# A second matrix product by one level of Strassen, softmax sums taken from the exponentials, and a new order table, in a fused graph-attention and slice-attention layer

## The chip, the cores and the metric

The kernel runs on one core of a Trainium2 chip. The metric is the device time of one execution in microseconds (us); the time before is the median of three runs. TensorE (PE) multiplies matrices out of SBUF into eight PSUM banks; its weight loads have a row of their own (PEld). VectorE (DVE) and ScalarE (ACT) do the elementwise work, GpSimd (POOL) a little, and SyncE (SP) issues nearly all transfers (DMA). Each engine runs its instructions in the order in which they are written.

## The reference, cut to what matters

There are 32 batches of 512 tokens with 256 features, all float32. A graph-attention block and a slice-attention block are each added to their input:

```python
# graph block on xn = layernorm(x)
out = relu(xn @ mlp1_w + mlp1_b)                  # 256 -> 512
residual = out
out = elu(gat(relu(out), None, W_fc, a_fc)) + residual
out = relu(out @ mlp2_w + mlp2_b)                 # 512 -> 256, the second mlp
residual = out
out = relu(elu(gat(relu(out), adj, W_hand, a_hand)) + residual)
x = x + out
# gat: h = inp @ W; e = leaky_relu(h @ a1 + (h @ a2).T), masked by adj; elu(softmax(e) @ h)

# slice block on xn2 = layernorm(x), 8 heads, 64 slices
slice_weights = softmax((x_mid @ W_slice + b_slice) / temp)   # over the 64 slices
slice_token = (fx_mid.T @ slice_weights) / sum(slice_weights)
attn = softmax(q @ k.T * scale); out_slice = attn @ v
x = x + (out_slice spread by slice_weights) @ W_out + b_out
```

## The kernel before, in words

Each batch goes through `front` (first layer norm, first mlp, first attention), `middle` (second mlp, second attention, residual) and `back` (second norm, slice softmax, slice attention, output). A batch is small, so the batches are pipelined: while one batch is in `back`, others are in `front` and `middle`, and their instructions are interleaved on every engine.

The interleaving is computed when the kernel is built. `nc` is a `Recorder` (line 105): every operation is noted with its engine, an estimated cost (`_cost`, line 182) and the tiles that it reads and writes. `_schedule` (line 226) then lets the engines take their next operation one by one, at each moment the one with the lowest key that could start, and respects data dependences and the number of buffers of each tag. The key (`order`, line 314) is `age * PERIOD + turn + shift`: `age` is the batch, `turn` comes from `TURNS`, which has a row of numbers for each step of the code (`nc.step = "mlp2"` and so on), and `shift` from `HEAD` and `TAIL`, which move whole steps of the first and last three batches. `SETUP` orders the preparation of the weights. `emit` (line 332) writes the instructions out in that order, and so each engine's queue has a fixed order. All recorded instructions therefore carry line 343 in the profile. Only in the first and last 120 us (in estimated time) does `emit` add fill matmuls on the identity (line 351) where TensorE would wait.

The steps that the change and the prediction touch:

- **The first attention** (`h` and `pv`, lines 761 to 902) already uses one level of Strassen in its two large products. There `product` makes one of seven products in a PSUM bank, and VectorE adds them up (`total`), with two copies by ScalarE (`keep`). `mix` and `pmix` hold the mixed operands.
- **o1** (line 902): the result comes back from a transposition by DMA into `o1T` (features on partitions, tokens on the free axis), and VectorE adds the residual.
- **mlp2** (line 912): `o2T = relu(w2.T @ o1T + b2)`, 256 features in two blocks of 128. Each block is four matmuls of 128 x 128 by 512 tokens, accumulated in one bank, then one ReLU with bias by ScalarE out of PSUM. The matmuls read `o1T` through `swapped` (line 477), which permutes the tokens on the way.
- **h2, e, p2, pv2** (lines 922 to 1008): the second, masked attention. `h2` projects `o2T`; `f2b` spreads one of the logits over a row; VectorE forms the masked rows `e` with their maxima `top`, ScalarE the exponentials, VectorE the maximum of both; the rows go out by `e_stage` and come back transposed in `p2T`. `pv2` multiplies and adds the residual into `x1`. `o2T` also goes out through `o2_stage`.
- **norm2** (line 1046): the second layer norm. The transposed rows come back by DMA into `xn2_raw`, which is a tile of the tag `o2T`: the same single buffer as the second mlp's output. ScalarE copies it into `xn2T`. (The profile shows the two names as `xn_raw` and `xn2T`.)
- **w** (line 1061): slice softmax. For each of four tiles of 128 tokens: logits of 512 columns in PSUM, the maximum of each of the 8 heads by VectorE (`mx`), 8 exponentials of 64 columns by ScalarE, the sums `rs` of the heads by a VectorE reduction over the 512 columns, their reciprocals, and a product.

In the first and last batch the transpositions are done by TensorE and not by DMA (`by_dma`, line 459), and `f2b` is copied out of PSUM.

Of the kernel before, what the change touches and what calls it, by code (L numbers as in the profile page):

```python
# [10 lines left out]
AF = mybir.ActivationFunctionType  # L11
OP = mybir.AluOpType
AX = mybir.AxisListType
# [1 line left out]
ENGINES = ("tensor", "vector", "scalar", "gpsimd", "sync")  # L15

TURNS = {
    "load": (-104.13,),
    "norm1": (5.81, -12.2, -0.38, 40.46, 5.49, 6.82, -28.3, -97.35, 73.26, 2141.3, -17.24, 7.8,
        -3.21, -61.78, -29.05, -31.03, -34.36, -3.93, -211.23, -208.37, -208.62, -207.57,  # L20
        -202.44),
    "mlp1": (44.88, -14.78, 475.5, -0.81, 29.84, 144.85, 30.48, 28.34, 46.7, 63.76, 30.7,
        163.15),
    "h": (217.43, 239.71, 301.88, 219.38, 228.31, 232.52, 223.78, 123.55, -183.63, -198.06,
        235.55, 281.78, 134.23, 84.93, 296.28, 284.15, 228.15, 213.81, 208.35, 40.76, -192.43,
        -208.97, 324.43, 90.08, 232.1, 162.36, 264.44, 305, 269.96, 302.11, 159.39, 131.88,
        217.06, 97.44, 286.09, 265.51, 197.21, 172.48, 330.83, 139.13, 316.66, 332.6, 199.8,
        210.03, 184.56, 233.17, 252.5, 357.26, 288.33, 243.5, 272.56, 242.46, 243.89, 262.61,
        301.12, 303.21),
    "factors": (1172.98, 68.61, 957.87, 880.81, 833.88, -94.89, 162.9, 564.16, 443.05, 632.16,  # L30
        99.22, 41.55, 117.2, -36.09, 151.35, 166.12, 162.03),
    "p": (-217.52, 222.09, -214.68, 156.3, -232.9, 226.84, -201.59, 222.19),
    "pv": (181.62, 173.02, 113.17, 168.75, 130.31, 121.86, 154.04, 91.05, 128.61, 93.43, 156.55,
        170.07, 249.5, 203.18, 183.65, 209.43, 161.93, 146.07, 129.44, 175.77, 84.33, 98.64,
        193.99, 67.43, 82.92, 77.34, 188.5, 225.33, 179.85, 196.17, 141.96, 66.83, 209.82,
        122.72, 185.96, 166.17, 256.1, 208.95, 191.25, 109.15, 168.68, 33.05, 111.29, 31.79,
        223.06, 225.68, 0.25, 146.41, 143.11, 131.52, 150.56, 135.14, 171.77, 185.87, 148.08,
        129.9, 112.28, 230.93, 210.68, 202.98, 108.67, 123.15, 135.98, 121.57, 427.87, 287.12,
        306.19, 126.95, 47.96, 44.6, 23.6, 354.94, 212.32, 233.37, 145.94, -25.73, 89.65, 87.01,
        301.3, 340.74),  # L40
    "o1": (175.72, 146.36, 318.31, 75.22, 202.48, -123.71, -11.06, -130.7, -287.11),
    "mlp2": (163.2, 216.89, 255.93, 271.92, 60.63, 285.36, 184.81, 130.74, 28.96, 65.99),
    "h2": (154.01, 126.18, 171.55, 124.34, 108.59, 78.41, 169.3, 89.79, 186.32, 157.35, 180.91,
        192.19, 105.96, 124.57, 26.13, 58.76),
    "e": (226.55, 172.24, 227.68, 199.08, 187.7, 234.17, 190.31, 206.45, 237.64, 232.92, 168.72,
        256.08, 408.52, 421.68, 391.27, 262.45, 442.54, 455.27, 273.82, 234.38, 519.53, 170.71,
        164.48, 31.36),
    "p2": (-14.68, 22.01, 55.59, 61.1, 56.92, -11.8, 67.6, 558.07, 85.28, 48.17, 40.53, 30.86,
        19.78, -12.55),
    "pv2": (231.3, 86.58, 94.48, 97.84, -101.11, 186.76, 109.51, 61.52, 85.01, -131.77, -150.14,  # L50
        205.52, 259.66, 267.31, 237.42, -131.44, -160, -120.69, -132.24, 154.68, 148.6, 111.83,
        139, -129.21, 152.77, 106.35, 144.25, 119.14, -162.13, -156.66, 273.74, 322.31, 325.93,
        361.68, -139.88, -151.25, -142.85, -161.55),
    "norm2": (3024.02, 107.62, 108.82, 88.2, 97.55, 53.73, 74.18, 49.61, 117.29, 3167.28,
        180.18, 68.34, 64.85, 86, 21.41, 8.51, 60.74, 13.84, 28.42, 83.96, 129.51, 212.73,
        234.97, 261.11, 2822.4, 116.47),
    "w": (305.34, 272.53, 290.14, 845.93, 798.64, 795.47, 283.65, 884.75, 926.27, 320.18, 751.4,
        375.01, 408.12, 405.42, 336.46, 305.77, 323.75, 367.7, 1201.11, 1138.46, 1563.38,
        745.63, 1124.55, 865.97, 1179.02, 980.75, 363.54, 428.69, 395.78, 437.6, 334.39, 367.5,
        367.07, 981.88, 934.2, 840, 174.53, 1035.96, 203, 1037.78, 1034.98, 480.9, 411.92,  # L60
        442.36, 358.87, 346.56, 246.11, 386.64, 1234.45, 758.39, 808.64, 610.85, 681.86, 882.99,
        492.47, 722.21, 414.99, 446.77, 335.28, 249.32),
    "sums": (219.1, 219.58, 227.77, 239.7, 383.95, 249.92, 251.57, 239.42, 242.03, 1077.37,
        1977.83, 234.3, 1454.25, 735.43, 2640.86, 592.26, 423.25, 660.64, -9.73),
    "s1T": (108.57, 368.64, 346.43, 140.99, 183.21, 126.3),
    "tokens": (328.88, 276.03, 298.43, 280.34, 354.01, 226.15, 295.4, 216.36, 344.5, 310.56,
        213.27, 259.2, 166.72, 280.67, 245.65, 277.29, 211.49, 312.02, 299.07, 271.19, 138.52,
        257, 235.11, 203.31, 251.8, 264.98, 212.57),
    "att": (205559.95, 208057.13, 394.33, 51833.74, 297.35, 190333.7, 260689.92, 418216.35),
    "vo": (374.47, 235.14, 638.61, 320.05, 321.87, 373.17, 345.11, 230.64, 163.72, 211.34,  # L70
        232.93, 232.76, 169.48, 276.17, 419.48, 556.46),
    "gg": (-50.95, -63.34, -63.34, -51.08, -78.74, -66.07, -40.3, -20.46, 150.92, 121.98),
    "out": (158.85, 78.08, -2.92, 6.88, -44.11, -73.16, -25.26, -4.67, 103.63, 87.34, -10.37,
        24.58, -12.49, 48.01, 59.4, 101.43, 136.08, 81.21, 268.69),
}
PERIOD, SPARE = 80.54, 0.01

HEAD = (
    (-61, -359, 0, 40, 0, 69, -1262, 189, -43, 457, -8, -24, 143, 947, 108, 718, -48, 6, 1, -39,
     119, -20),  # L80
    (168, 1, 0, 0, 0, 4, 174, 0, 144, -26, 75, 433, 58, 166, 0, 117, 154, 0, -183, -48, -372,
     1721),
    (172, 728, 1325, 0, -59, -269, -21, 34, -18, -363, 2035, 398, 404, -24, 1613, -199, 25,
     -134, 0, -3, -46, -85),
)
TAIL = (
    (36, 0, -352, 1, 67, 0, -772, 105, -24, 0, -312, 50, -6, -235, 1896, 375, 54, 83, -211, 13,
     -147, -271),
    (18, -170, -262, -383, 0, 42, 11, -11, -950, 795, -14, -10, -1671, -108, -157, 653, 6, 18,
     0, 210, 2, 652),  # L90
    (-4, -40, 0, -69, 10, -43, -630, -53, 276, -593, -1, -10, -589, 151, 299, 42, 316, 15, 89,
     4, -160, 43),
)


SETUP = (791.3598735632129, 2808.359873563213, 4385.359873563213, 9205.359873563213, 6407.359873563213, 3020.359873563213, 4840.359873563213, 5931.359873563213)

FLIPPED = ("xn", "u", "e", "o2", "w", "xn2")

P = 128  # L100
# [290 lines left out]
def adj_ffn_kernel(  # L391
# [26 lines left out]
    B, N, D = x.shape  # L418
    HID = mlp1_w.shape[1]
    HH = HID // 2  # L420
    NT = N // P
    KD = D // P
    KH = HID // P
    HEADS = temperature.shape[1]
# [12 lines left out]
    def ts(i, n=P):  # L437
        return slice(i * n, (i + 1) * n)

    def new(name, shape, bufs=1, tag=None, dtype=F32):  # L440
        return sbuf.tile(list(shape), dtype, name=name, tag=tag or name, bufs=bufs)

    def mm_tile(shape):
        return psum.tile(shape, F32, tag="bank", name="mm", bufs=8)
# [32 lines left out]
    def swapped(cols):  # L477

        return cols.rearrange("p (t a i) -> p a t i", t=NT, i=Q)
# [4 lines left out]
    def row(name, shape=(P, 512), tag=None):  # L484
        return new(name, shape, bufs=2, tag=tag)

    def small(name, shape):
        return new(name, shape, bufs=3)
# [74 lines left out]
    nc.step = "setup0"  # L563
    w2 = new("w2", [P, KH, D])
    nc.sync.dma_start(w2, mlp2_w.rearrange("(k p) f -> p k f", p=P))
    b2 = new("b2", [P, KD])
    nc.sync.dma_start(b2, mlp2_b.rearrange("(m p) -> p m", p=P))

# [341 lines left out]
    def middle(b, o1T):  # L910

        nc.step = "mlp2"
        o2T = new("o2T", [P, KD, N])
        for m in range(KD):
            pm = mm_tile([P, N])
            for k in range(KH):
                nc.tensor.matmul(
                    pm.rearrange("p (a t i) -> p a t i", t=NT, i=Q), w2[:, k, ts(m)],
                    swapped(o1T[:, k, :]), start=(k == 0), stop=(k == KH - 1),
                )  # L920
            nc.scalar.activation(o2T[:, m, :], pm, AF.Relu, bias=b2[:, m : m + 1])
        nc.step = "h2"
        h = new("h2", [P, NT, D + 2], tag="h" if b == B - 1 else None)
        for t in range(NT):
# [7 lines left out]
        for j in range(NT):  # L932
            nc.tensor.transpose(f2b[:, ts(j)], h[:, j, D + 1 : D + 2].to_broadcast([P, P]), ident)
        if not by_dma("e", b):
            pt, f2b = f2b, new("f2b", [P, N], tag="acb")
            nc.scalar.copy(f2b, pt)
        nc.step = "e"
        pT = new("p2T", [P, NT, N], tag="pT" if b == B - 1 else None)
# [105 lines left out]
    def back(b, x1):  # L1044
# [21 lines left out]
        for t in range(NT):  # L1066
# [7 lines left out]
            pm3 = pm.rearrange("p (h g) -> p h g", g=G)  # L1074
            mx = small("mx", [P, HEADS])
            nc.vector.tensor_reduce(mx, pm3, axis=AX.X, op=OP.max, negate=True)
            for hd in range(HEADS):
                nc.scalar.activation(w3[:, hd], pm3[:, hd], AF.Exp, bias=mx[:, hd : hd + 1])
            rs = small("rs", [P, HEADS])
            nc.vector.tensor_reduce(rs, w3, axis=AX.X, op=OP.add)  # L1080
            nc.vector.reciprocal(rs, rs)
            nc.vector.tensor_tensor(
                w3, w3, rs[:, :, None].to_broadcast([P, HEADS, G]), op=OP.mult
# [206 lines left out]
```

## Time and profile before

| | |
|---|---|
| Median of three runs | 2467.51 us (2467.47 to 2471.15) |
| The profiled execution, its own time | 2464.71 us |
| Its span, first to last instruction | 2462.9 us |
| Instructions in the span | 35296 |
| Granted TensorE clock, mean | 1.00 |
| ScalarE: exponentials of `w` | 1024 of 128 x 64, 231.1 us busy |
| Fill matmuls | 128 + 56 + 6, 26.1 us busy |
| TensorE busy before 374.58 us, and after 2167 us | 363.28 of 374.58, 287.27 of 295.90 us |

A span is counted from the first to the last instruction; a run's time is a little longer. In the lists of groups a line gives the code line, the engine, the operation, the tiles (out<-in), the shapes, the number of instructions, their busy time and mean duration in ns, and the idle time of the engine just before them with what ended it. A float32 matmul appears as two records, since it is made in two passes. In the list of instructions in order of time a line has the start in us, the length of the stretch in us, and then engine and tiles.

### The profile page before, as it was taken

Reading aid. Unit: us, or ns where it says so; the run is one execution under the profiler, and the core shown is the slowest. Engines: PE = TensorE matmul, PEld = TensorE weight load, DVE = VectorE, ACT = ScalarE, POOL = GpSimd, SP = SyncE. Lnnn points to the kernel's source line nnn. Section 1 sums busy time; section 2 is a strip of 40 time slices with the busy share of each in tenths; the row PEclk is TensorE's granted clock in tenths of the full one; section 3 lists DMA queues with packets and bytes.
Section 4 is the critical chain, followed back from the end, with each engine's and each line's share of the span. In section 5 each row is a group of like instructions: output and inputs, shape, how many; then the busy total and the mean of one; then the engine's idle time right before and its main releaser. Section 6 shows DMA issues by size and latency. Waiting matters only on the chain.

```text
span 2462.9 us, 35296 instructions
## 1 busy us (share of the span) xinstructions
PE 2442.5 (99%) x11607; PEld 1705.3 (69%) x11607; DVE 2096.1 (85%) x5636; ACT 1428.9 (58%) x3319; POOL 116.8 (5%) x184
## 2 busy tenths in 40 slices
PE   9999999999999999999999999999999999999999
PEld 7766667666676767676766676766767676767666
DVE  8688798888898888898888888888988888998775
ACT  2665556656556555566565566565565555665564
POOL 4000000000000000000000000000000000000000
PEclk9999999999999999999999999999999999999999
DMA  5133565455565455655555664556654556645531
GB/s 176 35 93 100 154 165 163 126 160 140 157 165 144 133 147 149 163 165 136 149 144 144 165 164 130 156 139 154 168 146 134 147 150 161 163 127 143 139 106 54
DMA packets 450047, 348.11 MB, mean 141 GB/s; under 512 B 109381, under 2 KB 374469, under 8 KB 449864
## 3 DMA queue, kind: packets, MB, share of 16 engines
q1 hardware_dynamic: 449334, 345.85, 51.8%
q8 instruction: 92, 1.51, 0.2%
q14 instruction: 91, 0.75, 0.1%
q10 hardware_dynamic: 530, 0.01, 0.0%
HBM read 186.27 MB, written 159.45 MB: 140 GB/s over the span
## 4 chain that ended last, share of the span: by engine, by line
PE 86%; DVE 3%; DMA 2%; ACT 0%; issue 0%; SPq 0%; DVEq 0%
PE mm L343 83%; PE tr L343 3%; DMA p2T<-scr 1%; DVE e L343 0%; DMA rn<-line 0%; DVE v L343 0%; DMA o1T<-scr 0%; SPq L343 0%; DVE e_stage L343 0%; DVE gg L343 0%; DMA scr<-e_stage 0%; DVE mx L343 0%; DVE pT L343 0%; DVE rs L343 0%; DVE xn_stage L343 0%
## 5 line engine op out<-in xcount | busy, mean ns | idle before, releaser
L343 ACT ACTIVATE w<-mm,mx 128x64 f32<-128x64 f32 x1024 | 231.1, 346 | 41.7 <-DVE mx L343 41.7
L343 PE MATMUL mm<-weff,xn2T 128*128 128x512 f32 x512 | 247.2, 598 | 0.5 <-ACT xn2T L343 0.5
L343 PE MATMUL mm<-w,xn 128*128 128x512 f32 x512 | 235.9, 593 | 3.5 <-DVE w L343 3.5
L343 PE MATMUL mm<-o1T,w 128*128 128x512 f32 x512 | 235.1, 593 | 1.3 <-DVE o1T L343 1.3
L343 PE MATMUL mm<-h,p2T 128*128 128x257 f32 x1024 | 232.5, 380 | 0.9 <-DMA p2T<-scr 0.9
L343 PE MATMUL mm<-gg,wT 128*128 128x256 f32 x1024 | 231.4, 382 | 0.2 <-DVE gg L343 0.2
L343 PE MATMUL mm<-xnT,w 128*128 128x512 f32 x512 | 225.9, 593 | 0.5 <-ACT xnT L343 0.4
L343 PEld LDWEIGHTS mm<-h,p2T 128*128 128x128 f32 x1024 | 193.7, 189 | 42.5 <-issue 14.5
L343 PEld LDWEIGHTS mm<-gg,wT 128*128 128x128 f32 x1024 | 190.0, 190 | 46.4 <-DVE gg L343 22.1
L343 ACT ACTIVATE v<-v,rd 128x512 f32<-128x512 f32 x128 | 90.5, 713 | 172.9 <-DVE rd L343 172.9
L343 PEld LDWEIGHTS mm<-xnT,w 128*128 128x128 f32 x512 | 96.9, 190 | 119.2 <-issue 111.2
L343 ACT ACTIVATE above<-e,top 128x512 f32<-128x512 f32 x128 | 88.4, 720 | 126.1 <-DVE top L343 109.4
L343 PEld LDWEIGHTS mm<-w,xn 128*128 128x128 f32 x512 | 96.1, 190 | 87.9 <-issue 72.3
L343 PEld LDWEIGHTS mm<-o1T,w 128*128 128x128 f32 x512 | 94.6, 190 | 85.9 <-issue 73.4
L343 PEld LDWEIGHTS mm<-weff,xn2T 128*128 128x128 f32 x512 | 93.8, 189 | 70.4 <-issue 56.4
L343 PEld LDWEIGHTS mm<-h,pT 128*128 128x128 f32 x512 | 96.3, 189 | 64.6 <-issue 37.9
L343 ACT ACTIVATE m<-m,neg 128x512 f32<-128x512 f32 x192 | 137.3, 717 | 1.3
L343 PE MATMUL mm<-h,pT 128*128 128x257 f32 x512 | 134.6, 380 | 3.4 <-DVE pT L343 3.4
L343 DVE TENSOR_TENSOR v<-mm,v 128x256 f32<-128x256 f32 (+1 forms) x320 | 127.7, 409 | 3.5 <-PE mm L343 1.7
L343 PE MATMUL mm<-wh,o2T 128*128 128x258 f32 x512 | 127.4, 382 | 0.0
L343 PE MATMUL mm<-h,pmix 128*128 128x256 f32 x512 | 125.8, 378 | 0.0
L343 PE MATMUL mm<-wfc,o0T 128*128 128x257 f32 x512 | 125.0, 385 | 0.0
(191 smaller groups left out, 5002.2 us busy)
## 6 DMA issues: line engine op xcount, KB each, us to landing
scr<-xn_stage SPq DMA_DIRECT2D x240, 128.0 KB, 3.0
scr<-u_stage SPq DMA_DIRECT2D x120, 256.0 KB, 4.4
o1T<-scr SPq DMA_DIRECT2D x30, 1024.0 KB, 7.6
scr<-e_stage SPq DMA_DIRECT2D x120, 256.0 KB, 4.3
p2T<-scr SPq DMA_DIRECT2D x30, 1024.0 KB, 5.4
scr<-w_stage SPq DMA_DIRECT2D x120, 256.0 KB, 4.0
w_raw<-scr SPq DMA_DIRECT2D x30, 1024.0 KB, 7.8
x<-in_x_dram SPq DMA_DIRECT2D x32, 512.0 KB, 4.2
```

Of the source, the lines that this page charges most:

```text
L343: getattr(getattr(self.nc, op.engine), op.method)(*op.args, **op.kwargs)
```

## The change

Three things are changed.

1. **The second mlp** is computed by one level of Strassen (in the form with few additions). `w2` is cut into four blocks of 256 x 128 and `o1T` into four of 256 x 256. Seven products of two matmuls (128 x 128 by 256 tokens) each go to a PSUM bank of their own. Three mixed blocks of `w2` go to a new tile `mixed2`, two are formed in place, once, in the preparation. The four mixed blocks of `o1T` are formed by VectorE in every batch, in the buffer of `p2T`. Two products are copied by ScalarE into parts of `o2T`, VectorE adds up the rest there with seven additions, and ScalarE does ReLU and bias in place in four parts. The permutation of the tokens is now in the places that are written in `o2T`.
2. **The sums of the slice softmax** are put out by the exponentials themselves (`accum_out`), 8 for each tile, in place of the reduction `rs` by VectorE.
3. **The order**: `TURNS`, `PERIOD`, `HEAD`, `TAIL` and `SETUP` have new values throughout, and the rows of `mlp2` and `w` other lengths. The copy of `f2b` in the edge batches moves to the buffers of tag `u`.

```diff
-PERIOD, SPARE = 80.54, 0.01
+PERIOD, SPARE = 75.16, 0.01
...
     w2 = new("w2", [P, KH, D])
     nc.sync.dma_start(w2, mlp2_w.rearrange("(k p) f -> p k f", p=P))
+    mixed2 = new("mixed2", [P, 3, 2, P])
+    w2_11, w2_12, w2_21, w2_22 = (w2[:, ts(k, 2), ts(m)] for m in range(KD) for k in range(2))
+    m1, m2, m4 = (mixed2[:, i] for i in range(3))
+    for to, left, op, right in (
+        (m1, w2_21, OP.add, w2_22), (m2, m1, OP.subtract, w2_11), (m4, w2_12, OP.subtract, m2),
+        (w2_21, w2_11, OP.subtract, w2_21),
+    ):
+        nc.vector.tensor_tensor(to, left, right, op=op)
+    m3 = w2_21
+    nc.vector.tensor_scalar(w2_22, w2_22, -1.0, None, op0=OP.mult)
...
         nc.step = "mlp2"
         o2T = new("o2T", [P, KD, N])
-        for m in range(KD):
-            pm = mm_tile([P, N])
-            for k in range(KH):
-                nc.tensor.matmul(
-                    pm.rearrange("p (a t i) -> p a t i", t=NT, i=Q), w2[:, k, ts(m)],
-                    swapped(o1T[:, k, :]), start=(k == 0), stop=(k == KH - 1),
-                )
-            nc.scalar.activation(o2T[:, m, :], pm, AF.Relu, bias=b2[:, m : m + 1])
+        o11, o12, o21, o22 = (o1T[:, ts(k, 2), ts(n, 2 * P)] for k in range(2) for n in range(2))
+        mix = new("mix2", [P, 4, 2, 2 * P], tag="p2T")
+        t1, t2, t3, t4 = (mix[:, i] for i in range(4))
+        for to, left, right in ((t1, o12, o11), (t2, o22, t1), (t4, t2, o21), (t3, o22, o12)):
+            nc.vector.tensor_tensor(to, left, right, op=OP.subtract)
+
+        def product(left, right):
+            pm = mm_tile([P, 2 * P])
+            for k in range(2):
+                nc.tensor.matmul(pm, left[:, k, :], right[:, k, :], start=(k == 0), stop=(k == 1))
+            return pm.rearrange("p (t a i) -> p t a i", t=2, i=Q)
+
+        def part(m, n):
+            return o2T[:, m, :].rearrange("p (a t i) -> p t a i", t=NT, i=Q)[:, ts(n, 2)]
+
+        def total(to, left, right):
+            nc.vector.tensor_tensor(to, left, right, op=OP.add)
+
+        c11, c12, c21, c22 = (part(m, n) for m in range(2) for n in range(2))
+        nc.scalar.copy(c12, product(w2_11, o11))
+        total(c11, product(w2_12, o21), c12)
+        nc.scalar.copy(c22, product(m1, t1))
+        total(c12, product(m2, t2), c12)
+        total(c21, product(m3, t3), c12)
+        total(c12, c12, c22)
+        total(c22, c21, c22)
+        total(c12, product(m4, o22), c12)
+        total(c21, product(w2_22, t4), c21)
+        for m, n, c in ((0, 0, c11), (1, 1, c22), (0, 1, c12), (1, 0, c21)):
+            nc.scalar.activation(c, c, AF.Relu, bias=b2[:, m : m + 1])
...
-            pt, f2b = f2b, new("f2b", [P, N], tag="acb")
+            pt, f2b = f2b, row("f2b", tag="u")
...
+            rs = small("rs", [P, HEADS])
             for hd in range(HEADS):
-                nc.scalar.activation(w3[:, hd], pm3[:, hd], AF.Exp, bias=mx[:, hd : hd + 1])
-            rs = small("rs", [P, HEADS])
-            nc.vector.tensor_reduce(rs, w3, axis=AX.X, op=OP.add)
+                nc.scalar.activation(
+                    w3[:, hd], pm3[:, hd], AF.Exp, bias=mx[:, hd : hd + 1],
+                    accum_out=rs[:, hd : hd + 1],
+                )
             nc.vector.reciprocal(rs, rs)
```

## The prediction

> **What bounds the kernel now.** I read the page's busy shares first, then the chain that ended last, then one steady stretch cut out by the period that the chain shows.
>
> ```profile
> PE 2442.5 (99%) x11607; PEld 1705.3 (69%) x11607; DVE 2096.1 (85%) x5636; ACT 1428.9 (58%) x3319; POOL 116.8 (5%) x184
> PE 86%; DVE 3%; DMA 2%; ACT 0%; issue 0%; SPq 0%; DVEq 0%
> 374.58 63.52 PE mm L343 x278
> 449.26 63.52 PE mm L343 x278
> 1196.07:1270.75 74.68, 74.68 (x355) 51.91 (x357) 65.29 (x176) 44.26 (x104) 2.91 (x5) 1.00 0.56 150
> ```
>
> The second line is the chain by engine, the next two are pieces of the chain in order of time, and the last is a stretch with the busy time of PE, PEld, DVE, ACT and POOL. The chain repeats every 449.26 - 374.58 = 74.68 us: one batch. In that period TensorE has no idle time at all, VectorE has 74.68 - 65.29 = 9.4 us and ScalarE 30.4 us. So 32 x 74.68 = 2389.8 us of the span are TensorE's own work at one batch a period, and 2462.9 - 2389.8 = 73.1 us are filling and draining the pipeline of batches. The granted clock is 1.00.
>
> A busy matrix unit could still be slack in disguise, and the Trainium skill warns of it: Perfetto Trace Analysis, section "Identifying the Most-Contended Engine", holds matmul busy time to be a bad measure and takes the share of weight loads instead. By that reading TensorE stands at 69% and VectorE, at 85%, is the engine to relieve; this change loads VectorE by about 3.0 us a batch (below), so it would cost up to 32 x 3.0 = 96 us and end near 2560 us. The rows say otherwise: matmul starts follow each other at the streaming rate with no gap, and VectorE's idle time is waits for others, the largest of them for TensorE (last line of the next fence, from the waits between 500 and 2000 us). I go by the rows.
>
> **The second mlp on TensorE.** The price of a pass is the distance between starts, not the duration (durations overlap). From the instructions in order of time:
>
> ```profile
> 1185.52 5.32 PE L343 MATMUL mm<-o1T,w 128*128 128x512 f32 x12
> 1190.67 0.27 PE L343 MATMUL tr<-ident,fm 128*128 128x128 f32 x1
> 1139.41 3.63 PE L343 MATMUL mm<-hx,pmix 128*128 128x256 f32 x16
> 1142.88 1.03 PE L343 MATMUL mm<-h,pmix 128*128 128x256 f32 x4
> DVE mean L343 <- PE mm L343: 62.4, 20, 3.1
> ```
>
> Twelve 512-wide passes take 1190.67 - 1185.52 = 5.15 us, 0.429 each; sixteen 256-wide passes take 1142.88 - 1139.41 = 3.47 us, 0.217 each. A float32 matmul is two passes. Before: 2 x 4 matmuls, 16 passes x 0.429 = 6.87 us. After: 7 products x 2 matmuls, 28 passes x 0.217 = 6.08 us. **Gain 0.79 us a batch, 25.3 us in 32.** A rule speaks against halving the width: the same page, section "Matmuls", says that larger matmuls are more efficient. Here two halves cost 2 x 0.217 - 0.429 = 0.005 us more than a whole, 14 x 0.005 = 0.07 us a batch, already in the sum. Weight loads rise by 12 x 0.19 = 2.3 us a batch (of 51.9), but a load of 0.190 us still fits beneath a pass of 0.217. The operand is now read in plain order and the permutation moves to the writes: the swapped 512-wide pass (593 ns) costs no more than the plain one (593 in the first mlp), so nothing is gained or lost there.
>
> **VectorE.** The rows (groups by operation and shape):
>
> ```profile
> L343 DVE TENSOR_REDUCE rs<-w 128x8 f32<-128x512 f32 x128 | 83.1, 667 | 1.8 <-ACT w L343 1.8
> L343 DVE TENSOR_TENSOR mix<-o0T 128x512 f32<-128x512 f32 x64 | 45.0, 705 | 3.3 <-ACT o0T L343 3.1
> L343 DVE TENSOR_TENSOR v<-mm,v 128x256 f32<-128x256 f32 x192 | 77.8, 411 | 1.8 <-PE tr L343 1.0 <-PE mm L343 0.3
> L343 ACT ACTIVATE o2T<-mm,b 128x512 f32<-128x512 f32 x64 | 43.8, 688 | 60.4 <-PE mm L343 59.5
> L343 ACT ACTIVATE w<-mm,mx 128x64 f32<-128x64 f32 x1024 | 231.1, 346 | 41.7 <-DVE mx L343 41.7
> L343 ACT ACTIVATE ex<-ex 128x8 f32<-128x8 f32 x32 | 6.6, 208 | 21.3 <-DVE ex L343 17.4 <-DVE h L343 3.9
> L343 DVE DVE_READ_ACCUMULATOR2_ANT top<- 128x1 f32 x128 | 10.6, 83 | 0.0
> ```
>
> Added per batch: 4 subtractions of 512 at 45.0/64 = 0.70 (2.8 us) and 7 sums of 256 at 0.41 (2.9 us). Removed: 4 reductions for the softmax sums at 83.1/128 = 0.65 (2.6 us). Net +3.0 us: VectorE goes to about 68.3 us of a period of 74.68 - 0.79 = 73.9, 92%. The cover is its 9.4 us of idle time, of which 5.6 stay; uncovered it would cost 96 us. The sums wait for products, and VectorE runs in order, so whatever follows (the combinations of the first attention, the masks of the second) waits too. The 14 products of the first attention's projection do the same today, and the waits of their sums total 14.9 us over 20 batches, 0.75 us a batch; for 7 products I expect 0.4. That fits in 5.6.
>
> **ScalarE.** Two ReLUs of 512 at 0.69 go (-1.4), two copies of 256 at 0.40 and four in-place ReLUs of 256 at about 0.46 (the 256-wide scaled copy into `u` is 458 ns) come (+2.6). The sums from the exponentials have no row: nothing extra if the sum comes free, and if it is a read-out of its own, between 83 ns (VectorE's, last line) and 208 ns (ScalarE's smallest instruction). I take 200 ns, nearest to the row of the same engine: 32 x 0.2 = 6.4 us. ScalarE goes to 44.3 + 1.2 + 6.4 = 52 us of 73.9; even the upper end has 20 us of cover, so the steady price is zero. A tile's softmax gets longer by 8 x 0.2 - 0.65 = 1 us, and keeps its PSUM bank 1.6 us longer; TensorE's waits for `w` are 3.5 us in the whole run today.
>
> **Storage and queues.** `mix2` lives where `p2T` does. In one period `p2T` is last read by a pass that ends about 1159.7, the second mlp runs 1182.6 to 1190.7, and the next transfer into `p2T` is issued at 1220.4: 23 us free on one side, 30 on the other. No wait. No transfer is added; those of SP keep their count and only take another order. The mixing of `w2` is five VectorE instructions once (about 2 us, in a first stretch of 62 us where VectorE has 10 idle). The mask row of the edge batches moves to another buffer, twice in the run: nothing.
>
> **The store `o2T`** is the one place without visible room. Its users follow each other: ReLU of the second mlp, second attention, residual, second norm, whose transposed data land in the same buffer, and then the next batch's ReLU.
>
> ```profile
> 1185.99 0.62 ACT L343 COPY xn2T<-xn_raw 128x512 f32<-128x512 f32 x1
> 1187.59 0.60 ACT L343 COPY xn2T<-xn_raw 128x512 f32<-128x512 f32 x1
> 1188.22 0.69 ACT L343 ACTIVATE o2T<-mm,b 128x512 f32<-128x512 f32 x1
> 1190.87 0.69 ACT L343 ACTIVATE o2T<-mm,b 128x512 f32<-128x512 f32 x1 [1.96 <-PE mm L343]
> ```
>
> The new ReLU starts 0.03 us after the last copy out of the old content: the loop through this buffer takes the whole period. Today its first write to its last is 1191.56 - 1188.22 = 3.3 us. Afterwards the first write is the copy of the first product and the last a ReLU after the seventh: 6 x 0.87 + 0.4 + 0.5 + about 0.4 of handing over = 6.5 us. The loop gets 3.2 us longer, and the period 0.8 shorter, so 4.0 us must be found in it. There are: ScalarE waits 3.8 us for the row maxima `top` of the masks, where the four mask instructions are interleaved with other work, and from the last pass of the second attention (1159.7) to its residual's end (1170.5) 10.8 us pass for some 4.7 us of its own instructions. About 10 us can be taken out by order alone, and the order is what the new table sets. I put the steady price at zero.
>
> **Edges.** The first and last batches are not covered by others. There the 3.2 us of the longer mlp and some 1 us of the longer softmax stand open, and 2 us of `w2`; fill matmuls (26 us busy) and 20.4 us of idle TensorE show that these ends wait on latency already. Both ends at full price are 2 x 4.2 + 2 = 10, wholly hidden 0. I take 5.
>
> **Sum.** Profiled execution: 2462.9 - 25.3 + 5 = 2442.6 of span, and with the 1.8 us around it (2464.71 against 2462.9) 2444.4. The median of the runs, 2467.51, lies 2.8 above the profiled execution, so the forecast is **2447 us**.
>
> **Rivals.** *VectorE stalls TensorE in part* (chance 0.20): at 92% an in-order engine delivers some operands late. For it speaks that one of its waits today is 3.1 us long every batch and can't be filled by will; against it that 5.6 us remain. A stall of 0.2 to 0.7 us a batch leaves 3 to 19 us of the gain: 2449 to 2464. *The `o2T` loop becomes the bound* (0.10), the case that ends slower: if the order finds less than about 3.2 us in the loop, the period rises above 74.68 by what is missing, 31 us per us; with nothing found, 31 x 3.2 + 5 = +104 us, 2570. At 1 us missing it is 2504. *The new order of the edges is better* (0.12): the 46 us of fill and idle time there can shrink by 5 to 15: 2430 to 2440. *The change doesn't do what it says* hardly exists: the number of passes is fixed by the code; it fails only if a 256-wide pass with another weight each time cost more than 0.2455 us (6.87/28), and the row has 0.217 with a new weight each time.
>
> **How the numbers follow.** The gain is kept: 0.58 (2440 to 2454 by the edges' bounds). With the rivals: faster by over 0.2% (below 2462.6; about what a measurement here tells from none) 0.58 + 0.12 + 0.16 = 0.86; within 0.2% 0.04; slower 0.10. The range 2432 to 2464 leaves out the slower case and the best tail of the edges.
>
> **What would show it.** Right: a period near 73.9 in the chain, TensorE without idle time in it, 28 passes of 0.217 for the mlp, VectorE near 68 us a period, ScalarE near 52 with read-outs as instructions of their own or longer exponentials, `xn2T` copies done before the first product's copy into `o2T`. Wrong: waits of PE or PEld on VectorE's `o2T` or `mix2`; a period above 74.7 with the `o2T` chain through it; or more than 80 us outside the 32 periods.

## The result, and the profile after

| | before | after |
|---|---|---|
| Median of the runs, taken side by side | 2468.22 us | 2447.71 us (2447.05 to 2449.21) |
| The profiled execution, its own time | 2464.71 us | 2448.21 us |
| Its span | 2462.9 us | 2446.4 us |
| Period (one batch) | 74.68 us | 73.775 us |
| Span outside 32 periods | 73.1 us | 85.6 us |

The ratio is 0.9916, with a 95% interval from 0.9898 to 0.9933: 20.5 us less. The forecast was 2447 us. That it was met within 1 us is in part luck, since three of its terms were off and their errors cancel. The period fell by 0.905 us where 0.79 was forecast (29.0 us in 32 batches for 25.3: 3.7 better). The time outside the 32 periods rose by 12.5 us where 5 was forecast (7.5 worse). And the median, put 2.8 us above the profiled execution, lay 0.5 below it (3.3 better).

First the page of the kernel after: the busy times by engine, and the share of each engine in the chain that ended last.

```profile
PE 2422.8 (99%) x11999; PEld 1784.0 (73%) x11999; DVE 2176.1 (89%) x5865; ACT 1581.2 (65%) x4471; POOL 118.8 (5%) x184
PE 94%; DVE 3%; DMA 1%; POOL 1%; issue 0%; ACT 0%; SPq 0%; DVEq 0%; ACTq 0%; POOLq 0%
```

Then, from the chain in order of time (start, length, what), the same place in two batches that follow each other: 453.08 - 379.31 = 73.77 us; the mean over 22 batches is 73.775.

```profile
379.31 67.44 PE mm L344 x316
453.08 67.45 PE mm L344 x316
```

One period cut into two stretches (busy time of PE, PEld, DVE, ACT and POOL, then granted clock, DMA share and GB/s):

```profile
1264.10:1297.30 33.20, 33.20 (x155) 23.37 (x154) 33.18 (x88) 25.96 (x81) 1.74 (x3) 1.00 0.50 150
1297.30:1337.90 40.60, 40.60 (x212) 30.90 (x211) 34.40 (x97) 23.29 (x59) 1.26 (x2) 1.00 0.59 154
```

TensorE has no idle time in either. VectorE is idle for 6.2 us of the period, but all of it lies in the second stretch; in the first it works for 33.2 us without a gap. The experiments come back to this.

Some instructions of the second mlp in order of time (start, length, what):

```profile
1324.58 1.46 PE L344 MATMUL mm<-o1T,w 128*128 128x256 f32 x6
1325.88 1.46 PE L344 MATMUL mm<-mix,mixed 128*128 128x256 f32 x6
1327.17 0.59 PE L344 MATMUL mm<-mix,w 128*128 128x256 f32 x2
```

From start to start, six passes take 1.30 and 1.29 us: 0.216 us each. Four of the groups that are new (instructions, busy time, mean ns, idle time before them):

```profile
L344 ACT ACTIVATION_READ_ACCUMULATOR w<-mm,mx 128x1 f32 x1024 | 224.8, 220 | 0.0
L344 DVE TENSOR_TENSOR o2T<-mm,o2T 128x256 f32<-128x256 f32 x160 | 64.3, 418 | 9.2 <-PE mm L344 7.0 <-ACT o2T L344 1.4
L344 ACT ACTIVATE o2T<-o2T,b 128x256 f32<-128x256 f32 x128 | 61.1, 504 | 87.8 <-DVE o2T L344 87.6
L344 DVE TENSOR_TENSOR mix<-o1T 128x512 f32<-128x512 f32 x64 | 41.2, 684 | 0.0
```

The sum put out by an exponential is an instruction of its own on ScalarE, 220 ns long. The sums of products wait little for TensorE (7.0 us in 160 instructions). The first row of `mix` is half of the subtractions; two more groups of 32 have the same mean of 684 ns.

### The profile page after: what moved, and what is told of

Same layout as the page of the kernel before. It is cut to its first block, busy times and chain, and to the rows that moved or that the text cites. A ratio compares the mean times of both kernels' runs of the same rounds, so it can differ in the third digit from the quotient of the medians.

```text
span 2446.4 us, 37809 instructions
## 1 busy us (share of the span) xinstructions
PE 2422.8 (99%) x11999; PEld 1784.0 (73%) x11999; DVE 2176.1 (89%) x5865; ACT 1581.2 (65%) x4471; POOL 118.8 (5%) x184
## 4 chain that ended last, share of the span: by engine, by line
PE 94%; DVE 3%; DMA 1%; POOL 1%; issue 0%; ACT 0%; SPq 0%; DVEq 0%; ACTq 0%; POOLq 0%
PE mm L344 91%; PE tr L344 3%; DVE e L344 0%; POOL mbias L344 0%; DVE m L344 0%; DMA wfc<-in_L_gnn_W_fc_dram 0%; DMA rn<-line 0%; DMA p2T<-scr 0%; DVE pT L344 0%; DVE xn L344 0%; DVE xn_stage L344 0%; DMA xn_raw<-scr 0%; DVE v L344 0%; DVE mx L344 0%; DMA b<-in_L_gnn_mlp_b_dram 0%
## 5 line engine op out<-in xcount | busy, mean ns | idle before, releaser
L344 ACT ACTIVATE w<-mm,mx 128x64 f32<-128x64 f32 x1024 | 309.2, 328 | 58.6 <-DVE mx L344 57.0
L344 PE MATMUL mm<-weff,xn2T 128*128 128x512 f32 x512 | 260.5, 605 | 1.4 <-ACT xn2T L344 0.7
L344 PE MATMUL mm<-w,xn 128*128 128x512 f32 x512 | 228.4, 593 | 1.0 <-DVE w L344 1.0
L344 ACT ACTIVATION_READ_ACCUMULATOR w<-mm,mx 128x1 f32 x1024 | 224.8, 220 | 0.0
L344 ACT ACTIVATE o0T<-mm,b 128x512 f32<-128x512 f32 x128 | 87.5, 686 | 98.8 <-PE mm L344 98.8
L344 ACT COPY q<-mm 128x256 f32<-128x256 f32 x32 | 11.9, 372 | 198.7 <-PE mm L344 198.5
L344 PE MATMUL mm<-wfc,mix 128*128 128x257 f32 x512 | 132.0, 379 | 0.5 <-DVE h L344 0.5
L344 PE MATMUL mm<-h,pT 128*128 128x257 f32 x512 | 121.4, 380 | 1.7 <-DVE rs L344 0.9
L344 PE MATMUL mm<-mixed,mix 128*128 128x257 f32 x512 | 121.9, 379 | 0.0
L344 ACT ACTIVATE m<-m 128x512 f32<-128x512 f32 x192 | 119.8, 625 | 2.2
```

The lines of the kernel that those rows point to most:

```text
L344: getattr(getattr(self.nc, op.engine), op.method)(*op.args, **op.kwargs)
```

## The experiments

The theory (A): the period is TensorE's own work; the gain is what the mlp's passes take less, and nothing else moved into the way. The rivals: (B) it is the new order that gains, and the mlp little; (C) VectorE's cover is smaller than its idle time says, and the softmax sums had to go for the mlp's additions to fit; (D) the loop through `o2T` is just short of the bound. And for the ends: (E) they are longer because the mlp's and softmax's chains are longer there, or because of the order of the preparation.

In most kernels the order of after is kept, and an operation is exchanged only as the instructions are written out. So the order of all others stays the same.

### The second mlp direct (e1), or with a product less (e3), with the order computed anew

```diff
-        c12, ... = seven products, nine combinations, four ReLUs
+        two blocks of four 512-wide matmuls and one ReLU, as in the kernel before
```

> The kernel after with its new table, but the second mlp as in the kernel before (the order is computed anew from the same table). Theory A, TensorE sets the period and the seven products are worth what their passes take: the period goes back from 73.77 to about 74.67 us, and the time rises by 32 x 0.90 = 29 us to about 2476, if the 85.6 us outside the periods stay. If the longer second mlp is what lengthened the ends (73.1 to 85.6), about 8 of these come back: 2468. Rival B, VectorE (67.6 us busy of 73.77) held the period up: with 5.6 us less on VectorE the period stays near 73.8 and the time near 2448.

```diff
-        total(c12, product(m4, o22), c12)
+        total(c12, c22, c12)
```

> The kernel after with one of the seven products left out (the one of m4 and o22; the sum takes another part in its place, so that VectorE has as many instructions). What is left out makes the second mlp wrong. Theory A: four passes of 0.216 us less, 32 x 0.86 = 27.6 us off, about 2420. Rival B or the loop through the buffer of o2T as the bound: the time stays within 8 us of 2447.7.

Measured: 2909.01 us (ratio 1.1793, 1.1775 to 1.1811) and 2911.95 us (1.1797, 1.1777 to 1.1817). Two opposite edits cost the same 460 us. The page of the direct one:

```profile
PE 2614.8 (90%) x11683; PEld 1764.8 (61%) x11683; DVE 2062.8 (71%) x5508; ACT 1512.8 (52%) x4343; POOL 113.5 (4%) x184
```

TensorE is idle for 10% of the span, and its mean granted clock is 0.94. The numbers of `TURNS` are laid over a step's operations by their place in the list, so with other operations each gets another's number. Both runs missed what was expected of them and say nothing about the mlp. They say that the table belongs to exactly these operations: with the order kept, the same two edits cost 47 us and gain 5 (e5 and e6, next).

### The second mlp direct, in the order of after (e5)

The plain mlp's matmuls stand in the places of the first four products; in the places of the last three there is one matmul of one column each. Subtractions, sums and copies are left out, and each ReLU reads its block out of PSUM. In the batches 1 to 3 the first block is begun ahead of the last residual addition into `o1T`, so a part of the mlp there lacks that residual; the work is the same.

```diff
-    product i: 2 matmuls of 256 on mixed operands, i = 0..6
+    i = 0..3: 4 matmuls of 256 on w2 and o1T;  i = 4..6: 1 matmul of 1 column
```

> The kernel after with its order kept, instruction for instruction, but the second mlp without Strassen: at the places of the first four products stand the 16 plain matmuls of 256 columns, the mixing and the adding by VectorE is left out, four ReLUs out of PSUM take the place of the copies and of the ReLUs in place, and one matmul of one column keeps each of the three banks that are no longer needed in turn. Theory A, TensorE sets the period: 4 passes more (0.86 us) and three small ones (0.1 to 0.3), period 74.7 to 74.9, time 2447.7 + 30 to 37 = 2478 to 2485 with the ends unchanged. Rival B, VectorE holds the period: 5.6 us less on VectorE, and the time stays within 10 us of 2447.7 or falls.

Measured: 2494.76 us (1.0111, 1.0096 to 1.0126). Its chain, two neighbouring batches:

```profile
1213.82 58.82 PE mm L367 x280
1289.12 58.82 PE mm L367 x280
```

The period is 75.30 us, 1.53 more than after, and TensorE waits for nothing. In it the one-column matmuls take 0.50 us from start to start (0.1 to 0.3 was expected, and mainly by this the time is above the 2478 to 2485 of theory A) and the 32 passes of the mlp 6.99 us. Less the 32 x 0.50 = 16 us that the direct mlp wouldn't have, it is 2479 us against 2447.7: the seven products are worth 31 us in this order, 0.97 a batch. This is theory A, and B falls: by this estimate the new order without the products would be slower than the kernel before.

### One product left out, in the order of after (e6)

```diff
-        product i = 5 (m4, o22): 2 matmuls
+        left out; its sum takes c22 in place of the product
```

> The kernel after in its own order with one product (m4 and o22) left out and another part of the sum in its place; the second mlp is then wrong. Theory A: 32 x 0.86 = 27.6 us off, about 2420. Rivals, VectorE or the loop through the buffer of o2T as the next bound just behind TensorE: less than half of it, 2434 or more. The earlier try of the same with a newly computed order told nothing of it, since the order itself cost 464 us.

Measured: 2442.40 us (0.9897, 0.9881 to 0.9914). If TensorE alone set the period, four passes less would have brought 4 x 0.216 = 0.86 us a batch, 27.6 us; they brought 5.3. The period is 73.59, only 0.18 less. Its chain shows what comes next:

```profile
1261.41 63.58 PE mm L348 x302
1325.01 0.42 DVE o2T L348
...
1326.77 0.34 DVE hx L348
...
1327.77 0.43 DVE o2T L348
...
1328.22 0.92 ACT o2T L348 x2
...
1329.18 2.88 PE mm L348 x12
```

From the mlp the path goes through VectorE's sums of `o2T`, with other instructions (`hx`) between them in its queue, and the last two ReLUs to the projection of the second attention. In the waits this is `PE mm <- ACT o2T`, 9.1 us in 21 times. So a further chain lies 0.18 us a batch behind TensorE. In the kernel after it is covered, but passes saved at this place would gain next to nothing more. The chain itself holds 69.4 us of TensorE's work in each period and 4.2 us of the others; passes saved in that work should shorten it too, which wasn't tried.

### The sums back to VectorE, in the order of after (e2)

```diff
-    nc.scalar.activation(..., AF.Exp, ..., accum_out=rs[:, hd : hd + 1])
+    nc.scalar.activation(..., AF.Exp, ...)
+    nc.vector.tensor_reduce(rs, w3, axis=AX.X, op=OP.add)   # ahead of the reciprocal
```

> The kernel after in its own order, instruction for instruction, but the sums of the slice softmax by a VectorE reduction just ahead of each reciprocal, and the exponentials without sums. VectorE gets about 2.6 us a batch, ScalarE loses 5.0. Theory A, the 6.2 us of idle time on VectorE cover it: period 73.8, time within 5 us of 2447.7. Rival B, VectorE is close to the bound or stalls TensorE when late: the period rises by 0.5 to 2.6 us, 2463 to 2530. In theory A this edit of the change was worth nothing by itself; in B it was needed to make room for the Strassen sums.

Measured: 2509.45 us (1.0168, 1.0153 to 1.0184), 62 us more than after: 1.9 us a batch for 2.6 us of work on an engine with 6.2 us of idle time. One of its shorter periods (the mean is 75.6), and the waits between 500 and 2000 us (engine waiting, for whom: total us, times, longest):

```profile
1170.95:1246.36 75.41, 74.30 (x363) 54.14 (x363) 70.11 (x188) 46.26 (x108) 3.00 (x5) 1.00 0.54 149
```

```profile
PE mm L348 <- DVE w L348: 13.4, 19, 0.7
PE mm L348 <- DVE gg L348: 8.0, 20, 0.4
```

TensorE waits for VectorE's rows now, and VectorE still has 5.3 us of idle time. Rival C holds in part: in this order the mlp's additions and the old reduction don't both fit; an order made for both wasn't tried. But the run can't tell whether it is the amount of work on VectorE or that the softmax's own chain (exponentials, sum, reciprocal, product) got later. The next one can.

### The same reduction on VectorE where nothing waits for it (e12)

```diff
     flip(wt, stage_w[:, :, ts(t, Q)])
+    nc.vector.tensor_reduce(spare, wt, axis=AX.X, op=OP.add)   # batches 1 to 30, never read
```

> Kernel after in its own order, with one further VectorE reduction of 512 columns behind each flip of w into its stage, in the batches 1 to 30; its result goes to a spare tile that nothing reads, so the output is the reference's. That is some 2.6 us of VectorE a batch, the same volume as in e2, where it stood ahead of the reciprocals and cost 2.0 us a batch. If place decides (the chain from the maximum to w's flip got later), the work here falls on idle time of VectorE (6.2 us a batch) and costs at most 0.5 us a batch: 2448 to 2463 us. If volume decides (VectorE's queue in order is full at some places of the period whatever is behind it), it costs about as much as in e2: about 2505 us.

Measured: 2489.62 us (1.0096, 1.0079 to 1.0113), 41.9 us more than after, 1.4 in each of the 30 batches. It lies between the two expectations. The two runs agree when the work is counted by what it adds to VectorE's busy time, in which overlaps count once: 2.2 us a period here, where the next instruction begins before the sum has ended, and 2.6 in e2 (from the stretch 500 to 2000 us). So 0.8 us of the 2.2 found room here, and 0.7 of the 2.6 there. Volume alone accounts for both runs, and hardly anything is left for the later chain of the softmax. Nobody waits for the added instructions, and still TensorE does, through what is queued behind them. The chain by engine, and a piece of it:

```profile
PE 63%; DVE 25%; DMA 6%; issue 3%; SPq 2%; ACT 1%; POOL 1%; DVEq 0%; POOLq 0%; ACTq 0%
```

```profile
1240.12 0.62 DVE w_stage L344
1240.74 0.57 DVE spare L346
...
1241.37 0.66 DVE v L344 x2
...
1243.06 0.73 ACT v L344
...
1245.38 5.06 DMA xnT<-scr
1250.49 27.47 PE mm L344 x106
```

The added sum stands in the path itself: behind it a piece of the first attention, then the issue of a transfer, and then the first mlp of a later batch. All four added sums of a batch fall into the stretch in which VectorE has no gap (in after 1264.10 to 1297.30, shown above). There they push back what follows. What stands open afterwards is only the part of the later idle time that isn't tied to something else. The waits between 500 and 2000 us in the kernel after, and in this one:

```profile
DVE hx L344 <- PE mm L344: 31.5, 21, 1.5
DVE mix L344 <- ACT o0T L344: 21.1, 21, 1.3
DVE rd L344 <- PE mm L344: 17.0, 40, 0.5
DVE ra L344 <- ACT sc L344: 13.9, 21, 0.7
DVE m L344 <- ACT m L344: 12.1, 20, 0.6
```

```profile
DVE hx L344 <- PE mm L344: 26.6, 20, 1.5
DVE m L344 <- ACT m L344: 19.9, 20, 1.0
DVE ra L344 <- ACT sc L344: 13.4, 20, 0.7
DVE mix L344 <- ACT o0T L344: 1.2, 3, 0.7
```

The waits of `mix` and `rd` were real cover: 1.0 and 0.8 us a batch go to nearly nothing (`rd` is no longer among the waits). That of `m` grows by 0.4, and those of `hx` and `ra` hardly move. I read these last ones as round trips, in which VectorE waits for an engine that waits for VectorE's own last result, and which move along with the delay; that is argued from the rows, not tried. What is measured is the reserve: 2.2 - 1.4 = 0.8 us of VectorE's 6.2 us of idle time were usable here.

### Only the sums, in the kernel before (e4)

```diff
-            nc.vector.tensor_reduce(rs, w3, axis=AX.X, op=OP.add)
+            accum_out of the exponentials, in the order of before
```

> The kernel before in its own order, instruction for instruction, with only the sums of the slice softmax put out by the exponentials and the VectorE reduction left out. Theory A, TensorE alone sets the period: 74.7 us and 2467 to 2470 us, no change. Rival: the longer softmax (8 x 0.2 - 0.65, about 1 us a tile) arrives late at the sums by TensorE, whose product with w follows the last tile closely: 0.5 to 2 us a batch more, 2484 to 2530. Rival: VectorE's relief of 2.6 us lets waits of TensorE fall: nothing, since there are none.

Measured: 2474.89 us (1.0031, 1.0019 to 1.0043), span 2472.5. Two neighbouring batches in its chain, then the same in the kernel before:

```profile
755.28 63.52 PE mm L347 x278
829.97 63.52 PE mm L347 x278
```

```profile
747.98 63.52 PE mm L343 x278
822.66 63.52 PE mm L343 x278
```

The period stays at 74.68: a VectorE with 2.6 us less to do gains nothing while TensorE is full, and ScalarE's read-outs cost nothing in the steady part. "No change" was expected; the 9.6 us of span are lost at the ends: 7.2 in the first four batches (755.28 - 747.98 = 7.3 already stands here) and some 2.9 in the last, less a single stall of some 0.5 us in the middle of before that doesn't come again. In this order the longer softmax lies open there.

### The ends: direct mlp (e7), no sums (e8), another order of the preparation (e9)

Three kernels in the order of after look for the 12.5 us. One has the direct mlp only in the batches 0 to 3 and 28 to 31 (there on weights that stay mixed), one leaves the sums of the exponentials out there (a constant takes their place), and one moves the five first operations of the slice weights ahead of the mask's preparation on GpSimd.

```diff
-    the batches 0..3 and 28..31 as the others
+    e7: plain matmuls in place of the products     e8: exponentials without accum_out
```

> As the run without Strassen in the kept order, but only in batches 0 to 3 and 28 to 31 (with the mixed weights as they are, so that the second mlp of these eight batches is wrong). It measures what the longer second mlp costs at the ends. If its latency is what lengthened the ends from 73.1 to 85.6 us, 4 to 8 us come back there against 8 x 1 us of more TensorE work: 2444 to 2452. If it isn't, the time is 2447.7 + 8 = 2456.

> The kernel after in its own order with the exponentials' sums left out in batches 0 to 3 and 28 to 31 (the reciprocals there read a constant; the softmax of these batches is wrong by a factor). It measures what the longer softmax costs at the ends. In the order of before, the sums alone cost 9.6 us of span, all of it at the ends; if that is so here, 6 to 10 us come back: about 2440. If the new order of the ends hides them: 2446 to 2448.

```diff
-    GpSimd: mask (setup3), then the slice weights' first operations (setup5)
+    GpSimd: the slice weights' first operations, then the mask
```

> The kernel after in its own order, but in the preparation GpSimd forms the mask behind the block of W_x and not ahead of it, and W_x is fetched ahead of the adjacency and not behind the row that waits for a buffer. In the profile of after TensorE waits 4.8 us for W_x and then runs at a granted clock of 0.78 to 0.88 from 30 to 50 us. If this is part of the 12.5 us that the ends lost, 2 to 6 us come back: 2442 to 2446. If the first attention's chain through VectorE sets the start anyway, nothing: 2447 to 2449.

Measured: 2457.87 us (0.9961, 0.9946 to 0.9976), 2447.44 us (0.9919, 0.9905 to 0.9934) and 2453.55 us (0.9951, 0.9938 to 0.9963), against 2447.71 for after. None is measurably shorter; e7 and e9 are 10 and 6 us longer, and e9 missed both of its expectations. The plain mlp at the ends costs 10 us. Its own passes and one-column matmuls there are 8 x 1.47 = 11.8 us by the measure of e5, so its shorter way through the batch can have won some 2 us at most: the seven products aren't what lengthened the ends by 12.5. Without the sums nothing changes, so in the new order the longer softmax is covered even there. And with the mask later TensorE's wait for the slice weights falls from 4.8 to 1.7 us, but another takes its place (`PE mm <- ACT u`, 6.9 us); the mask's place is not what cost the time, or not by itself. What the profile shows of the head is this, the stretches 30:40 and 40:50 of after and then of before (TensorE's busy time first, its granted clock third from the end):

```profile
30.00:40.00 10.00, 5.19 (x27) 4.50 (x28) 9.97 (x23) 0.00 (x0) 10.00 (x9) 0.88 0.52 148
40.00:50.00 10.00, 8.86 (x56) 8.22 (x55) 8.14 (x27) 5.08 (x10) 2.69 (x3) 0.78 0.25 61
```

```profile
30.00:40.00 10.00, 9.41 (x61) 8.21 (x59) 10.00 (x34) 1.58 (x5) 3.07 (x4) 1.00 0.80 187
40.00:50.00 10.00, 7.72 (x60) 7.15 (x59) 9.09 (x22) 4.91 (x8) 9.04 (x6) 1.00 0.38 107
```

GpSimd prepares the mask earlier in after (from 25.2 us, before 40.9) and `wx`, the slice weights that TensorE waits for, later (from 38.3 us, before 27.7). TensorE stands idle for half of one stretch, and in the next it runs at a clock of 0.78. If the matmuls done by 600 us are counted at each kernel's steady distances, some 8 us of the loss lie in the head and the rest in the tail. Idle time and all fill matmuls over the whole run are 4.9 us more (20.4 + 26.6 before, 23.6 + 28.3 after), and the lower clock of the head is an estimated 2.5 us (8.86 us of work at 0.78 and 5.19 at 0.88). For the other 5 us no single cause was found.

### The second norm later (e10, e11)

GpSimd's power of the second norm is done once more, or three times more, on the same tile.

```diff
     self.nc.gpsimd.tensor_tensor(rstd, ..., op=OP.pow)
+    1 or 3 times more: rstd to the power of 1
```

> The kernel after in its own order with one more small GpSimd instruction (1.16 us) in the second norm, between its statistics and its use, in every batch: the loop through the buffer of o2T gets 1.2 us longer, and no other engine gets work. In the profile of after the data of the second norm land about 1.9 us before ScalarE copies them. If that is the loop's slack: no change, 2447 to 2449. If the loop is the bound that lies just behind TensorE: 0.5 to 1.2 us a batch, 2463 to 2485.

> As the run before with three such instructions, 3.5 us in the loop. With 1.9 us of slack in the loop the period rises by about 1.6 us: 2447.7 + 31 x 1.6 = 2497. If the loop has more room than the profile shows (other waits on the way give way): 2448 to 2460.

Measured: 2452.35 us (0.9947, 0.9933 to 0.9960) and 2519.09 us (1.0216, 1.0201 to 1.0232). The added powers end 1.1 us and 3.3 us later than the one would. With 1.1 us the period stays at 73.77, and 4.6 us are lost at the ends, so that the time lies between the two expectations. With 3.3 us the period is 75.64, 1.87 more, so the reserve behind the second norm is some 1.4 us; a further 12 us are lost outside the periods, and the time is above what was expected. A period of the long one, and its waits between 500 and 2000 us:

```profile
925.34:1000.98 75.64, 74.04 (x364) 54.17 (x364) 67.64 (x184) 49.19 (x139) 6.02 (x8) 1.00 0.53 148
```

```profile
DVE xn L344 <- POOL ln_rstd L347: 40.3, 20, 2.0
PE mm L344 <- DVE mix L344: 32.0, 20, 1.6
```

TensorE doesn't wait for `o2T`, as rival D would have it. VectorE's in-order queue stands for 2.0 us at `xn`, `mix` of another batch is queued behind it, and TensorE waits for that.

## Why the prediction was right, point by point

- **The second mlp on TensorE: right, a little small.** Forecast 6.87 to 6.08 us, gain 0.79. From start to start, all passes of a period taken together, it is 6.96 to 6.04, gain 0.92. Halving the width cost nothing: 2 x 0.216 = 0.432 against a mean of 0.435. The 0.429 of a 512-wide pass was taken from an undisturbed stretch; next to matmuls of another tile shape a pass is up to 0.1 us longer (of the sixteen of before, the one ahead of the 64 x 64 `tok,q` takes 0.523). The slice logits (`weff,xn2T`) stand there in the new order and lose 0.39, and other groups win it back, so that the sum over all groups is 0.90. What the products are worth is shown by e5: 0.97 us a batch.
- **Row against rule: the row was right.** The section "Identifying the Most-Contended Engine" of the Trainium skill's page Perfetto Trace Analysis would have had VectorE relieved, by TensorE's share of weight loads (69%; the share of peak arithmetic, which it names beside it, was not worked out here). This change gave VectorE more work, and the time fell with TensorE's; and e4, which relieves VectorE alone, gains nothing in the period.
- **VectorE: the load was right, its cover was not.** The durations of the added and removed instructions sum to +3.1 us a batch (forecast +3.0); busy time rises from 65.29 to 67.57, since instructions overlap. The sums wait 0.2 us a batch for their products (0.4 was expected). "That fits in 5.6" came true, but not for its reason: of 6.2 us of idle time only 0.7 to 0.8 could be used by further work (e2, e12). The rival "VectorE stalls TensorE in part" didn't happen but was near: with the reduction kept, in this order, its work would have turned the gain into a loss (2509). The rival's range of 2449 to 2464 also leaves out the 5 us of the edges that the forecast has; with them it is 2454 to 2469.
- **ScalarE: right.** The sums are read-outs of 220 ns (200 was taken, 83 to 208 were the bounds, so the upper bound was too low). With the mlp's copies and ReLUs the durations rise by 7.0 + 1.4 - 0.6 = 7.8 us a batch (the exponentials got shorter, 346 to 328 ns), but they overlap: ScalarE's busy time went up by 5.0 to 49.25, not to 52. The steady price is zero (e4).
- **Storage and queues: right where it matters.** No wait for `mix2` or `p2T` appears in the period, and TensorE waits for no transfer. Others do: between 500 and 2000 us ScalarE waits 17.0 us for `w_raw` (63.7 before), and VectorE 9.9 us for `rn`, which it did not before.
- **The store `o2T`: right.** From the first write (1326.22) to the end of the last ReLU (1332.36) 6.1 us pass; 6.5 was forecast. The copy of the first product again starts 0.03 us after the last copy out of the old content (1326.19). The time was found where the forecast looked: ScalarE's wait for `top` fell from 3.8 to 0.9 us, and the way from the second attention's last pass to its residual's end from 10.8 to 5.3.
- **Edges: this step failed.** "Both ends at full price are 2 x 4.2 + 2 = 10, wholly hidden 0. I take 5." It was 12.5, above the upper bound, and the sign set for "wrong" (more than 80 us outside the periods) came true. The price was put on the longer chains; e7 and e8 show that these cost at most some 2 us and nothing there in this order. What remains is the order of the preparation and of the first and last batches itself, which was changed throughout and which the forecast held to be neutral; this is by exclusion, since the one change of it that was tried (e9) gained nothing. The rival "new order of the edges is better" had the wrong sign. Which of its places cost the 12.5 us stays open apart from the idle, fill and clock terms named above.
- **Sum: near by luck.** -29.0 + 12.5 in place of -25.3 + 5: the span fell by 16.5 us, not 20.3. That the median still met the forecast is due to the 2.8 us above the profiled execution, which were taken over from before.

## What to carry to other kernels

When the period is full TensorE work, count its passes from start to start, and take what they save times the number of periods; then look for the next chain, since here a further saving of 0.86 us a batch at the same place brought 0.18. Don't take an engine's idle time for its reserve: here 0.8 of VectorE's 6.2 us could be used. Look for the longest stretch without a gap, and be wary of gaps behind it that may wait for the engine's own results. A change of order must be priced at the ends by itself: here the ends lost 12.5 us, and the longer chains there explain at most 2.

## What the runs showed that was not expected

- VectorE at 92% of the period had a gap-free stretch of 33.2 us and 6.2 us of gaps, of which 0.8 were usable; sums that nothing reads raised its busy time by 2.2 us a batch and cost 1.4.
- The sum put out by an exponential is an instruction of its own (1024 of 220 ns, 224.8 us in all); it overlaps with others, so that ScalarE's busy time rose by 5.0 us a period where the durations sum to 7.8.
- Leaving out four of TensorE's passes at every batch (27.6 us) shortened the run by 5.3 us.
- Two opposite edits in the list of operations cost nearly the same, 461 and 464 us, with the order computed anew; with the order kept they cost 47 us and gained 5.
